# Three placements at the seam and the end of the convolution in a two-layer kernel: the second pass's w2 loads, the sums of w2, and the pace of the convolution

## The chip, the cores and the metric

The kernel runs on one core of a Trainium2 chip. The metric is the device time of one execution in microseconds (us); the profile comes from one further execution, recorded by the hardware profiler. Engines are called PE (TensorE), DVE (VectorE), ACT (ScalarE), POOL (GpSimd) and SP (SyncE, here only an issuer of DMAs). Everything is fp32.

## The reference, cut to what matters

The input x has the shape (2, 56, 56, 384): 6272 tokens of 384 channels. Two layers follow each other.

```python
# layer 0
x = x + neighborhood_attention(layer_norm(x))          # 12 heads, 7x7 windows, then a projection
y = layer_norm(x)
x = x + gelu(y @ w1 + b1) @ w2 + b2                    # 384 -> 1536 -> 384
# layer 1
h = layernorm(x)
p = h @ w_in + b_in                                    # 384 -> 768
local = depthwise_conv_3x3(p, k_conv)                  # 768 channels
mixed = 0.25 * (scan(local, rows) + scan(local, rows, reverse)
              + scan(local, columns) + scan(local, columns, reverse)) + local
mixed = layernorm(mixed)                               # over 768 channels
x = x + mixed @ w_out + b_out                          # 768 -> 384
x = x + gelu(layernorm(x) @ w1 + b1) @ w2 + b2         # own weights, 384 -> 1536 -> 384
# scan: y[i] = 0.6 * y[i-1] + 0.4 * v[i]
```

## The kernel before, in words

The tokens are 49 tiles of 128. After the attention stage, two passes go over groups of tiles. The first pass (`groups`, 13 of them, the first with one tile, the others with four) does the MLP of layer 0 and then `project_in`: it multiplies by w_in, adds the bias on ACT (L1539) and stores p, channels first, to a DRAM tensor `p_d` (L1546, on SP's queue). The second pass (`dgroups`, twelve of four tiles and one of one) does `project_out` (the product with w_out, with the layer norm of `mixed` folded in) and the MLP of layer 1. PE does all products; a hidden column is `columns` (L1205) with its copy `hidden` (L1216), a token tile is `tokens` (L1223).

The 3x3 convolution and the scans don't use PE. They run on VectorE, ScalarE and POOL's queue, beside the products of the end of the first pass and the first three groups of the second (`switch` is 3). Their work is cut into jobs. A `Band` (some lines of 128 channels) loads its part of `p_d` as `pt` (L1280, SP's queue), multiplies by the centre tap on ACT (`centre`, L1295, output `loc`), adds eight taps on VectorE (L1312), stores `loc` to `loc_d` and `mix_d` (L1320, SP's queue), scans both ways on VectorE (L1258 to L1262), scales on ACT (L1327) and accumulates into `mix_d` by an accumulating DMA on POOL's queue (L1331). A `Columns` job does the scans along the other axis: it loads `loc` (L1350), turns it on ACT (L1360), scans, turns back on ACT (L1378, output `mixed`) and accumulates. The layer norm of `mixed` needs `mix_d`, which `load_mix` loads (L1435; and the residual rows, L658).

The order is written out by hand: each engine and each DMA queue takes its instructions in the order in which the program emits them, and an instruction that waits holds all that is behind it on its engine. How the convolution is woven into the products is decided by class `Beside`: a product calls `beside.go(worth, own)` with estimated VectorE microseconds, and the class emits steps of the jobs until the debt is paid:

```python
        self.due += self.rate * worth - own
        while self.due > 0.0:
            step = self.step()
```

`beside.until(name)` emits all that is left up to a job. `rate` starts at 1.0 and is set where the last group of the first pass begins (`g == last`). The call `beside.until((1, NI - 1))` in the third group of the second pass, at its third token tile, closes the convolution.

Weights of the MLP are loaded by `weights(layer)` (L674), three DMAs of 768 KB each for w1 and for w2, on SP's queue. Layer 1's w1 goes out in the first pass, its w2 between the two passes, at the last `project_in`. ACT copies the turned and normed input of an MLP from PSUM with `channels` (L282, output `hT`); `add_row` (L1144) adds a bias row by an accumulating DMA on POOL's queue.

From the fourth group of the second pass on (`g >= switch`), the products are done as two-by-two blocks with seven products in place of eight. `hidden_by_seven` (L1657 to L1704) makes the hidden columns with sums of w1 (`more_of_w1`, L1625, on VectorE) and of the input (`sums_of_input`, L1638, `xsums`); its first three PSUM banks are opened by `open_banks` (L1237). `sums_of_hidden` (L1721 to L1723, on POOL) and four sums of w2 (`sums_of_w2`, L1715, each 128 x 1152 elements) feed `tokens_by_seven` (L1749 to L1795), the first product of which writes the bank that a tile of `project_out` has used. In these groups `project_out` takes a function `then(k)` that it calls behind each of its tiles k; its evacuation is on VectorE (L1508), its layer norm's statistics are taken on VectorE by 32x32 transposes (L1460), and the norm of the result is closed behind the last tile. `turned` (L1188) transposes the normed result on VectorE for the next group, and L1195 scales it.

Of the kernel before, what the change touches and what calls it, by code (L numbers as in the profile page):

```python
# [178 lines left out]
def block_kernel(ctx: ExitStack, tc: tile.TileContext, ins: dict, out: bass.AP):  # L179
    nc = tc.nc  # L180
# [187 lines left out]
    hT = ep.tile([P, NC, PAIR], F32, name="hT")  # L368
# [26 lines left out]
    def channels_of(n, c, bank):  # L395
        tp = bank()
        for k in range(NT):
            turn_x(n, k, c, tp)
        return lambda: take_x(n, c, tp)
# [226 lines left out]
    def project(t, bank):  # L626
        ps = bank()[:, :C]
        at = t % 7 * P
        for c in range(NC):
            nc.tensor.matmul(  # L630
                ps, lhsT=ogs[t // 7][:, c, at : at + P], rhs=wproj[:, c, :],
                start=c == 0, stop=c == NC - 1,
            )

        def add():
            if t in loaded:
                add_bias(t)
            nc.vector.tensor_tensor(xrs[t], ps, xrs[t], ALU.add)
            stores.append(("x1", x1f[t * P : (t + 1) * P, :], xrs.pop(t)))
            if t + 3 < T2 // P - 4:  # L640
                load.append(t + 3)
        return add
# [149 lines left out]
    class Dense:  # L792
# [22 lines left out]
        def step(self, j):  # L815

            due, final = self.total * (j + 1) / self.steps, j == self.steps - 1
            if self.turns and self.jobs and self.before_turns <= 1 and self.n + 3 in normal:
                self.was = True
            while True:  # L820
                ready = len(to_project) > (2 if self.n == ng - 1 else 0)
                project_next = ready and not (self.jobs and (self.was or self.n == END))
                if not project_next and not self.jobs:
                    break
                w = VAL if project_next else self.jobs[0][0]
                if self.done + 0.5 * w > due and not (final and self.jobs):
                    break
                self.done += w
                self.was = project_next
                if project_next:  # L830
                    project(to_project.pop(0), next_bank)()
                else:
                    self.jobs.pop(0)[1]()()
                    self.before_turns -= 1
            while self.turns and self.before_turns <= 0 and self.n + 3 in normal:
                channels_of(self.n + 3, self.turns.pop(0), next_bank)()
                if not final:
                    break
# [26 lines left out]
    for t in range(NS + 2):  # L865
# [17 lines left out]
        for s in fresh:  # L883
            if s % UG == 0:
                dense = Dense(s // UG)
            if s == NU - UG - 4:
# [3 lines left out]
                w1, w2, w_parts = weights(0)  # L890
# [211 lines left out]
    def passes(xs, xn, w1, w2, between=lambda ps: None):  # L1102
# [10 lines left out]
        beside = Beside()  # L1113
# [86 lines left out]
        def columns(w, m, hT, n):  # L1200

            name = "uz" if ps_m is ps_u else "mm"
            ps = ps_m.tile([P, MT], F32, name=name)
            for c in range(NC):
                nc.tensor.matmul(  # L1205
                    ps[:, : n * P], lhsT=w[:, c, m * P : (m + 1) * P], rhs=hT[:, c, : n * P],
                    start=c == 0, stop=c == NC - 1,
                )
            return ps
# [321 lines left out]
        sum_steps, seeds = [], []  # L1531
        bands = [(b, lo, hi) for b in range(B) for lo, hi in BANDS[b]]

        def project_in(g, hT, between=lambda: None, at=1):
            t0, n = groups[g]
            pt = io.tile([P, NI, MT], F32, name="mx")
            for m in range(NI):
                ps = columns(w_in, m, hT, n)
                nc.scalar.activation(  # L1539
                    pt[:, m, : n * P], ps[:, : n * P], AF.Identity, bias=col("L1_conv_b_in", m)  # L1540
                )
                beside.go(MLP)
                if m == at:
                    between()
            for b, at, here, n in images(t0, n * P):
                nc.sync.dma_start(  # L1546
                    out=p_d[b][:, :, at : at + n].rearrange("m p t -> p m t"),
                    in_=pt[:, :, here : here + n],
                )
            while bands and bands[0][0] * T1 + min(bands[0][2] + 1, H) * W <= t0 + groups[g][1] * P:  # L1550
                b, lo, hi = bands.pop(0)
                beside.jobs += [Band(b, m, lo, hi) for m in range(NI)]
                if hi == H:
                    beside.jobs += [Columns(b, m) for m in range(NI)]
# [152 lines left out]
        def sums_of_w2(w2, engine=nc.gpsimd):  # L1707

            q = NHID // 2
            b11, b12 = w2[:, :q, : C // 2], w2[:, :q, C // 2 :]  # L1710
            b21, b22 = w2[:, q:, : C // 2], w2[:, q:, C // 2 :]
            t1, t2, t3, t4 = (tp.tile([P, q, C // 2], F32, name=f"w2_t{i}") for i in range(4))
            steps = []
            for to, x, y in ((t1, b12, b11), (t2, b22, t1), (t3, b22, b12), (t4, b21, t2)):
                steps.append(lambda to=to, x=x, y=y: engine.tensor_tensor(to, x, y, ALU.subtract))  # L1715
            return (t1, t2, t3, t4), steps
# [98 lines left out]
        hT = channels(xn, groups[0][1], "L0_conv_ln2_g", "L0_conv_ln2_b")  # L1815
        add_row(x, groups[0][1], "b2_0")

        for g, (t0, n) in enumerate(groups):
# [19 lines left out]
            if g == last:  # L1838
                beside.until((0, NI - 1))
                load_row(0, "b2_1")  # L1840
                ahead = load_mix(0)
                beside.rate = 0.98
            if g < last:
                x_next, n_next = xs.pop(g + 1), groups[g + 1][1]
                norm_next = Norm(sm) if g < EARLY.stop else Ready(g + 1)
# [96 lines left out]
            if early:  # L1942
                hT = io.tile([P, NC, MT], F32, name="hT")
            elif 0 < g < last:
                hT = channels(xn_next, n_next, *ln2)
# [28 lines left out]
            if g == 0:  # L1974
                hT = channels(xn_next, n_next, *ln2)
                xsums = sums_of_input(hT)
                w2_sums, sum_steps = sums_of_w2(w2)
# [11 lines left out]
        g, x2, norm_w = waiting  # L1989
# [6 lines left out]
        hT = channels(xn, groups[g][1], *n1)  # L1996
# [5 lines left out]
        norm.shift(dgroups[0][1])  # L2002
        ahead = load_mix(1)
        w2 = w2_1
        for part in w_parts[3:]:
            part()
        project_in(g, hT, first_input)
        n2 = "L1_conv_n2_g", "L1_conv_n2_b"

        hT = channels(first["xn"], dgroups[0][1], *n2)  # L2010
        add_row(x3, dgroups[0][1], "b2_1")
        for g, (t0, n) in enumerate(dgroups[:switch]):
# [15 lines left out]
            for k in range(n):  # L2028
                if k == n - 1:
                    hT = channels(xn, dgroups[g + 1][1], *n2)  # L2030
# [20 lines left out]
        ps_y, ps_u, bank_b, banks_b = open_banks(pctx, "tail")  # L2051
        ps_m = ps_u
        xsums = sums_of_input(hT, nc.vector)
        w2_sums, sum_steps = sums_of_w2(w2)
        for step in sum_steps:
            step()
        for g, (t0, n) in enumerate(dgroups):
            if g < switch:
                continue
            if g == dlast:  # L2060
                hid = [hidden(w1, m, hT, n, "L1_conv_b1") for m in range(NHID)]
                for k in range(n):
                    ps = tokens(hid, w2, k, y_end)
                nc.vector.tensor_copy(rows[:, 1, :], x3[:, n - 1, :])
                assert n == 1 and t0 + n * P == T2
                break
            n_next = dgroups[g + 1][1]
            add_row(ahead[1], n_next, "b_out")
            s1, s2 = (tp.tile([P, NHID // 2, MT // 2], F32, name=x) for x in ("s1", "s2"))
            low, high, finish = hidden_by_seven(  # L2070
                hT, xsums, w1, w1_sums, (s1, s2), measure_by_steps(ahead, range(min(n_next, 3))),
                "L1_conv_b1",
            )
            ahead[2].close(min(n_next, 3))
            more = measure_by_steps(ahead, range(3, n_next))

            def then(k):
                if k == 0:
                    finish()
                next(more, None)  # L2080
                if k == 1 and n_next > 3:
                    ahead[2].close(n_next, first=3)

            res = x3
            x3, norm = project_out(g + 1, *ahead, then)
            if g + 2 <= dlast:
                ahead = load_mix(g + 2)
            hT = io.tile([P, NC, MT], F32, name="hT")
            for i, _ in enumerate(tokens_by_seven(low, high, s1, s2, w2, w2_sums, res, res)):
                if i == 0:  # L2090
                    norm.shift(n_next)
                    xn = normalized(norm, x3, n_next)
                if 1 <= i <= n_next:
                    turned(xn, i - 1, hT)
                if i == 5:
                    scaled(hT, n_next, *n2)
                    xsums = sums_of_input(hT) if n_next == NT else None
                    add_row(x3, n_next, "b2_1")
            nc.sync.dma_start(
                out=yout[t0 : t0 + NT * P, :].rearrange("(k p) c -> p k c", p=P), in_=res  # L2100
            )
# [8 lines left out]
    with tc.If(again > 0):  # L2110
        attention_again()
        w1, w2, w_parts = weights(0)
# [81 lines left out]
```

## Time and profile before

| | |
|---|---|
| median of three runs | 2571.08 us (2569.76 to 2578.67) |
| the profiled execution | 2575.12 us |
| its span on the core | 2573.2 us, mean granted PE clock 0.995 |
| PE busy | 2531.9 us (98%) |
| DVE busy | 1985.1 us (77%) |
| ACT busy | 1137.9 us (44%) |
| POOL busy | 585.9 us (23%) |
| waits of PE from 1600 us on | 6.2 us at 1654, 1.6 us at 1860, 3.5, 1.8 and 3.1 us between 1909 and 1930, and 1.7 us in the other three |

In the profile's lines, a name such as `L1205` is the line of the kernel before; `hT L282 <- ...` or `[6.18 <-ACT hT L282]` gives an idle time and what ended it; `SPq` is SP's DMA queue at the moment of issue; PE's granted clock is a share of full speed, and the DMA share is the mean busy share of the core's sixteen DMA engines. The first pass ends near 1660 us, the convolution near 1920 us.

### The profile page before, as it was taken

The page shows a single profiled execution, that of the slowest core. Times are in us where ns is not written, and L with a number is a line of the kernel's source. Part 1 is how long each engine was busy: PE and PEld are TensorE (multiplying, and loading weights), DVE is VectorE, ACT ScalarE, POOL GpSimd, SP SyncE. Part 2 cuts the span into 40 slices and gives each one's busy share as a digit, 9 for nine tenths or more (in the row PEclk, how much of TensorE's full clock was granted, in tenths as well). Part 3 has the DMA queues.
Part 4 walks back from the last instruction along what each step waited for, and adds up shares of the span by engine and source line. Part 5 has one row for each costly group of instructions (what it writes and reads, how often), then busy time and mean ns, then how long its engine had stood idle before and what let it go on. Part 6 is the DMA issues. An engine that isn't in the chain of part 4 may idle for free. (4 is left out here: it accounts for less than half of the span.)

```text
span 2573.2 us, 41869 instructions
## 1 busy us (share of the span) xinstructions
PE 2531.9 (98%) x16678; PEld 1734.4 (67%) x16678; DVE 1985.1 (77%) x3702; ACT 1137.9 (44%) x2058; POOL 585.9 (23%) x622
## 2 busy tenths in 40 slices
PE   9999999999999999999999999899989999999999
PEld 5666666666698887455545555455558888888888
DVE  4888978887554453899989998789887877878871
ACT  5655655654443344334455444332862233233222
POOL 0111211111442331010110002121133333333332
PEclk9999999999999999999999999999999999999999
DMA  7423454225522223467677667956890333333210
GB/s 232 152 86 99 159 174 157 86 87 195 155 65 80 68 68 95 141 175 209 178 214 281 209 186 214 250 147 168 209 238 15 74 74 74 74 74 74 47 28 21
DMA packets 155597, 342.97 MB, mean 133 GB/s; under 512 B 11158, under 2 KB 112000, under 8 KB 153088
## 3 DMA queue, kind: packets, MB, share of 16 engines
q1 hardware_dynamic: 124096, 255.65, 29.6%
q0 software_dynamic: 26352, 57.81, 13.2%
q10 hardware_dynamic: 4944, 26.74, 3.1%
q8 instruction: 133, 2.18, 0.4%
q14 instruction: 72, 0.59, 0.1%
HBM read 176.39 MB, written 134.88 MB: 121 GB/s over the span
## 5 line engine op out<-in xcount | busy, mean ns | idle before, releaser
L1312 DVE SCALAR_TENSOR_TENSOR loc<-pt,taps,loc 128x495 f32<-128x495 f32 (+13 forms) x288 | 372.9, 1295 | 35.0 <-ACT loc L1295 26.5
L1205 PE MATMUL mm<-hT,w 128*128 128x512 f32 x720 | 317.6, 596 | 6.2 <-ACT hT L282 6.2
L581 ACT ACTIVATE pts<-pts 119x448 f32<-119x448 f32 (+5 forms) x396 | 210.8, 573 | 110.6 <-DVE pts L571 100.6
L571 DVE TENSOR_TENSOR pts<-sc,bias 119x448 f32<-119x448 f32 (+5 forms) x396 | 219.0, 615 | 45.1 <-PE sc L560 44.8
L1205 PEld LDWEIGHTS mm<-hT,w 128*128 128x128 f32 x720 | 135.1, 191 | 167.7 <-issue 155.5
L1188 DVE STREAM_TRANSPOSE hT<-xn 32x96 f32<-32x96 f32 x784 | 211.2, 269 | 27.7 <-ACT xn L265 17.5
L414 PE MATMUL ps<-hT,wqkv 128*128 128x448 f32 x504 | 204.8, 550 | 2.1 <-ACT vs L459 1.5
L1460 DVE STREAM_TRANSPOSE turned<-mx 32x192 f32<-32x192 f32 x528 | 194.8, 369 | 6.9
L1223 PE MATMUL y<-w,hid 128*128 128x384 f32 x552 | 181.9, 486 | 0.0
L1223 PE MATMUL y_end<-w,hid 128*128 128x384 f32 x552 | 181.8, 486 | 0.0
L1216 ACT ACTIVATE hid<-mm,chan 128x512 f32<-128x512 f32 x120 | 82.3, 685 | 161.3 <-PE mm L1205 161.3
L1223 PEld LDWEIGHTS y_end<-w,hid 128*128 128x128 f32 x552 | 104.6, 190 | 72.1
L1223 PEld LDWEIGHTS y<-w,hid 128*128 128x128 f32 x552 | 104.3, 190 | 71.3 <-issue 0.5
L414 PEld LDWEIGHTS ps<-hT,wqkv 128*128 128x128 f32 x504 | 91.3, 189 | 84.4 <-issue 74.2
L1205 PE MATMUL mm<-hT,w_in 128*128 128x512 f32 x324 | 140.7, 593 | 0.6 <-DVE hid_u L1676 0.6
L1657 PE MATMUL ua<-hT,w 128*128 128x256 f32 x504 | 123.4, 381 | 0.0
L1331 POOL DMA_DIRECT2D mix_d<-both x36 | 32.2, 894 | 397.0 <-ACT both L1327 327.1
L560 PEld LDWEIGHTS sc<-qT,kT 32*100 32x100 f32 (+3 forms) x3168 | 87.8, 169 | 47.3 <-DVE sum L590 7.6
L600 PE MATMUL o<-pts,vt 100*32 100x112 f32 (+3 forms) x3168 | 116.3, 263 | 1.2 <-ACT pts L581 1.2
L1664 ACT ACTIVATE hid<-hid_u,chan 128x256 f32<-128x256 f32 x168 | 76.1, 500 | 88.4 <-DVE hid_u L1676 68.8
L1205 PEld LDWEIGHTS mm<-hT,w_in 128*128 128x128 f32 x324 | 61.2, 190 | 77.2 <-issue 72.9
L237 POOL TENSOR_TENSOR rs<-rs,mhalf 128x4 f32<-128x4 f32 (+4 forms) x56 | 50.2, 897 | 272.2 <-DVE rs L234 271.1
(215 smaller groups left out, 5017.1 us busy)
## 6 DMA issues: line engine op xcount, KB each, us to landing
loc<-loc_d SPq DMA_DIRECT2D x24, 784.0 KB
xa<-x_d SPq DMA_DIRECT2D x24, 768.0 KB
xa<-rows POOLq DMA_DIRECT2D x24, 768.0 KB, 11.2
bias<-in_bias_t ACTq DMA_DIRECT2D x13, 1344.0 KB
p_d<-mx SPq DMA_DIRECT2D x11, 1536.0 KB
mx<-mix_d SPq DMA_DIRECT2D x11, 1536.0 KB
v_d<-vs SPq DMA_DIRECT2D x49, 192.0 KB
xr<-in_x SPq DMA_DIRECT2D x49, 192.0 KB
```

The costliest lines, as they stand in the source:

```text
L414: nc.tensor.matmul(ps, lhsT=wqkv[:, c, m * P : (m + 1) * P], rhs=hT[:, c, half_of(n)], start=c == 0, stop=c == NC - 1,)
L560: nc.tensor.matmul(sc[i // 2][: w.keys, i % 2, q : q + TT], lhsT=kT[d, hg, w.keys_at + r * w.kc : w.keys_at + (r + w.rows) * w.kc], rhs=qT ...
L571: nc.vector.tensor_tensor(self.pts[:n, h : h + 2, lo:hi, :], sc[half][:n, :, at * TT : (at + hi - lo) * TT].rearrange("p h (c q) -> p h c ...
L581: nc.scalar.activation(t, t, AF.Exp)
L600: nc.tensor.matmul(o[i * HD : (i + 1) * HD, self.slot, :TT], lhsT=w.vt[:n, c, h * HD : (h + 1) * HD], rhs=self.pts[:n, i, c, :], start=c = ...
L1188: nc.vector.transpose(hT[j : j + HD, :, k * P + i : k * P + i + HD], xn[i : i + HD, k, :].rearrange("p (c q) -> p c q", c=NC)[:, :, j : j ...
L1205: nc.tensor.matmul(ps[:, : n * P], lhsT=w[:, c, m * P : (m + 1) * P], rhs=hT[:, c, : n * P], start=c == 0, stop=c == NC - 1,)
L1216: nc.scalar.activation(t[:, : n * P], ps[:, : n * P], AF.Gelu, bias=col(b1, m))
L1223: nc.tensor.matmul(ps, lhsT=t[:, k * P : (k + 1) * P], rhs=w[:, m, :], start=m == 0 and onto is None, stop=m == len(lhs) - 1, skip_group_c ...
L1312: nc.vector.scalar_tensor_tensor(to, pt[:, lo + dy - self.top : hi + dy - self.top, xt : xt + n], self.tap(dy, dx), to, ALU.mult, ALU.add,)
L1460: nc.vector.transpose(t[j : j + HD].rearrange("p (m c) -> p m c", m=NI)[:, :, i : i + HD], mx[i : i + HD, :, k * P + j : k * P + j + HD],)
L1657: nc.tensor.matmul(bank[:, i, :], lhsT=w[:, m * P : (m + 1) * P], rhs=x, start=start and i == 0, stop=True, skip_group_check=True,)
```

## The change

It has three parts. The rate of the convolution's weaving is 1.0 instead of 0.98 from the last group of the first pass on. The three loads of layer 1's w2 are issued behind the last `project_in` and not ahead of it: on SP's queue they now stand behind the `pt` loads and stores that this `project_in` issues and behind its store to `p_d`, and ahead of the next two `pt` loads. And the four sums of w2 are made by VectorE instead of POOL, no longer at once where the seven-product groups begin, but one behind each of the four tiles of the first such group's `project_out` (in `then(k)`, behind `finish()` at the first of them).

```diff
@@ -1839,7 +1839,7 @@
                 beside.until((0, NI - 1))
                 load_row(0, "b2_1")
                 ahead = load_mix(0)
-                beside.rate = 0.98
+                beside.rate = 1.0
@@ -2002,9 +2002,9 @@
         norm.shift(dgroups[0][1])
         ahead = load_mix(1)
         w2 = w2_1
+        project_in(g, hT, first_input)
         for part in w_parts[3:]:
             part()
-        project_in(g, hT, first_input)
@@ -2051,9 +2051,7 @@
         xsums = sums_of_input(hT, nc.vector)
-        w2_sums, sum_steps = sums_of_w2(w2)
-        for step in sum_steps:
-            step()
+        w2_sums, sum_steps = sums_of_w2(w2, nc.vector)
@@ -2077,6 +2075,8 @@
             def then(k):
                 if k == 0:
                     finish()
+                if sum_steps:
+                    sum_steps.pop(0)()
                 next(more, None)
                 if k == 1 and n_next > 3:
                     ahead[2].close(n_next, first=3)
```

## The prediction

> **What bounds the kernel now.** First the page's shares, to see which engine sets the time.
>
> ```profile
> PE 2531.9 (98%) x16678; PEld 1734.4 (67%) x16678; DVE 1985.1 (77%) x3702; ACT 1137.9 (44%) x2058; POOL 585.9 (23%) x622
> ```
>
> TensorE (PE) works 98% of the span of 2573.2 us. Its matmuls are untouched, so only its idle and slow-clock time, 41.3 us of idle in all, can change. Second, PE's waits in the second pass and the seam before it (1600 us to the end; columns: total, times, longest):
>
> ```profile
> PE mm L1205 <- ACT hT L282: 6.2, 1, 6.2
> PE yb L1237 <- ACT hT L282: 3.5, 1, 3.5
> PE uz L1657 <- DVE hid_u L1704: 3.1, 1, 3.1
> PE ub L1657 <- ACT hid_u L1696: 1.8, 1, 1.8
> PE y_end L1223 <- ACT y_end L1487: 1.6, 1, 1.6
> ```
>
> The first lies at the seam, the fifth in dgroup 2, the rest where the convolution ends. None is later than 1940. Third, windows of 5 us around the first of them (PE, PEld, DVE, ACT, POOL busy; PE's granted clock; DMA share; GB/s):
>
> ```profile
> 1655.00:1660.00 5.00, 0.00 (x0) 0.00 (x0) 2.61 (x5) 1.55 (x3) 0.00 (x0) 0.68 1.10 309
> 1660.00:1665.00 5.00, 4.60 (x9) 2.16 (x10) 2.18 (x3) 1.81 (x4) 2.23 (x2) 0.63 1.07 323
> ```
>
> PE does nothing for 5 us, and then works at a granted clock of 0.63. The same dip follows the third wait (0.67 from 1930 to 1935) and the second; the waits of 1.6 and 1.8 us show none. In the matmuls' own lengths a dip is some 3.4 us at half speed, so a stall of 3 us or more costs about 1.7 us beyond itself. Fourth, the seam in the timeline (start, length, instruction, wait), SP's queue and then ACT:
>
> ```profile
> 1645.56 0.34 SPq L1280 DMA_DIRECT2D pt<-p_d  x1
> ```
>
> ```profile
> 1658.45 0.71 ACT L1295 ACTIVATE loc<-pt,taps 128x504 f32<-128x504 f32 x1 [4.82 <-DMA pt<-p_d]
> ...
> 1659.59 2.10 ACT L282 ACTIVATE hT<-tp,chan 128x512 f32<-128x512 f32 x3
> ```
>
> w2 (three loads of 768 KB, issued from 1636.72) is ahead of a 308 KB band load pt on SP's queue, which so takes 12.9 us. ACT waits for pt, and hT's copies are queued behind it on ACT. So PE's 6.18 us are w2's.
>
> **Part 1: w2 behind the project_in.**
> Gain: pt passes ahead of w2 and lands near 1648. ACT copies hT right behind PE's transposes (1653.65 to 1655.75), and hidden column 0 ends near 1657.0 instead of 1664.68: -7.7 us, the slow clock included.
>
> What is late next: the three loads now stand on SP's queue between the p_d store and the first band load whose loc is 128x1120 (issued at 1664.03 before, used by ACT at 1674.50). That load waits for p_d to land and is then behind w2. The nearest row is in the first pass, where three w1 loads follow a p_d store:
>
> ```profile
> 1589.31 0.37 SPq L1546 DMA_DIRECT2D p_d<-mx  x1
> 1589.78 3.08 SPq L674 DMA_DIRECT2D w<-in_L_conv_w  x3
> 1594.74 0.34 SPq L1280 DMA_DIRECT2D pt<-p_d  x1
> ```
>
> That pt was in use 13.9 us after p_d's issue. Here p_d goes out at 1654.8 to 1655.3 (1653.66 before; it is now behind stores that wait for VectorE's taps, done at 1654.2): pt at 1668 to 1670 by this row. But POOL's queue carries an accumulation of a band and two of rows (768 KB each) in the same time, and two queues share packet by packet. The queue lines of 1921 to 1926 show it:
>
> ```profile
> q0 software_dynamic: 377, 0.58, 65.5%
> q1 hardware_dynamic: 377, 0.77, 46.0%
> ```
>
> 1.8 MB at 0.58 MB in 5 us (0.116 MB/us) is 15 us of sharing, in which SP's queue gets 0.77/5 x 15 = 2.3 MB of its 4.8 MB (stores 0.25, p_d 1.57, w2 2.36, pt 0.6); the other 2.5 MB at about 0.39 MB/us (first-pass loads) take 6.4 us: 1655 + 15 + 6.4 = 1676. Another way: the DMA share is over 1 here, so the same bytes end later by the time in which the queue now lacks work, about 1649 to 1654: the load, landed at 1671.3 before, comes near 1676.5. I take 1677, with 1668 and 1680 as ends.
>
> ACT wants it after the third hidden column's copy, near 1663.5; PE has three banks and goes on to column 5, which ends at 1671.9. Then loc (1.22) and hid (0.69) run from 1677.0 to 1678.9, and column 6 starts at 1679.1, with 1.7 us of slow clock to follow: 1680.8 against 1679.5 before. So a 7 us stall replaces the 6 us stall. **Seam: +1.5 us** (from -7.7, if it lands by 1670, to +4).
>
> **Part 2: pace.** Rate 1.0 for 0.98 counts from 1541, where the second pass's work begins: 2% of 364 us is 7.3 us more convolution in the order by 1905. VectorE has room (41 busy of 50 us at 1850 to 1900). Two effects. In dgroup 2, seven ACT blocks of 3.1 us instead of six stand before the seeds of L1487, so y_end's wait of 1.57 becomes about 3.4: **+1.8** (0 to +4.5 with a slow clock). And at the end of the convolution fewer scans remain behind the last token tiles:
>
> ```profile
> 1907.62 3.12 ACT L1378 ACTIVATE mixed<-line 128x392 f32<-128x392 f32 x4 [3.54 <-DVE line L1262]
> ...
> 1910.54 2.07 ACT L282 ACTIVATE hT<-tp,chan 128x512 f32<-128x512 f32 x3
> ...
> 1912.43 3.81 DVE L1638 TENSOR_TENSOR xsums<-xsums,hT 128x256 f32<-128x256 f32 x1
> ...
> 1912.65 3.30 POOL L1715 TENSOR_TENSOR w_t<-w 128x1152 f32<-128x1152 f32 x1
> ```
>
> hT waited on ACT for a mixed block, that for a scan. With the last block ahead of hT, the 3.46 us go. The 1.82 us (ACT L1696 held for an accumulation of mix_d, 4.32) go because that leaves some 7 us earlier.
>
> **Part 3: sums of w2.** The four POOL subtractions go from there. VectorE's four xsums then take 4 x 0.43 = 1.7 us instead of 9.9 (1911.97 to 1921.86), L1704 comes early, and its 3.15 us go. With both slow stretches (1912.8 to 1916.2, 1929.9 to 1933.3; 1.65 each): 3.46 + 1.82 + 3.15 + 3.3 = **-11.7** (-7 to -12).
>
> Their new place is not free. A VectorE sum of 768 columns took 0.96 us (L1625), so 1152 columns take 1.43, four 5.7 us. VectorE last waits for PE at 1954.65 (L1676, 1.96); from there to the norm's close at 1967.80 it idles 0.7 us only. So the close comes 5.0 us later. L1508 of tile 2, done at 1965.04, is passed by two sums and ends near 1967.7, while PE wanted its bank at 1966.06: +1.7. Then xn, 64 transposes and L1195 run dense, and the first xsums (done 1993.11 on POOL, read by PE at 1994.23) comes at 1997.8, where PE after its first wait would read it at 1995.9: +1.9. **+4.2** with some 0.3 us of latency in each (+2 to +7).
>
> One rule speaks against this placing. The rows above: xsums went from 0.43 us (the first, at 1911.97) to 3.81 beside POOL's sum, and POOL's 2.8 us are what 1.27 us for 512 columns (L1721) scale to, so VectorE alone paid. The Trainium skill ("SBUF — State Buffer", section "SBUF: two separate sides") says that the shared port pair is locked for a whole instruction, and whichever starts second is blocked. By the page POOL's L1722 and L1723 (1955.19 to 1957.68) would also wait behind the first moved sum, 1.43 us each at most; by the row only VectorE waits, up to 1.2 us. Sum 4.2 without a meeting, 5.4 with one. I keep 4.2, as one of four sums meets them, and 7 as upper end.
>
> **Sum.** +1.5 +1.8 -11.7 +4.2 = -4.2 us on the profiled 2575.12 us (0.16%), whose span is 2573.2 with 1.9 around it. It lies between the runs' 2571.08 median and their highest, 2578.67, so I put the difference on the median: 2567.
>
> **Rivals.**
> (a) *No new stall at the band load.* POOL's rows finish early enough and pt lands by 1670. For: 13.9 us in the first pass. Against: the shared queues and a DMA share over 1. Seam -7.7: sum -13.4, 2557.7 (-10 to -19).
> (b) *Slower: w2 holds the band load.* Each us of landing after 1677 costs PE one. From 1681.2 on the change loses, from 1694 by over 12.9 us, the 0.5% that a measurement of this kernel can tell from no change. For: p_d goes out late and everything is behind it in one queue. Against: the bytes end near 1676 by two counts. At 1688: +7, 2578.
> (c) *The end doesn't move.* Extra pace turns into waits on ACT (L1360 and L1378 were already what scans waited for), so hT stays late; only the POOL sums' 3.15 + 1.65 go. +1.5 +1.8 -4.8 +4.2 = +2.7, 2574.
>
> **How the numbers follow.** Forecast 0.50 (2561 to 2574), (a) 0.20, (b) 0.18, (c) 0.12. The range 2553 to 2583 takes in (a) but its far end, and (b) up to a landing of 1693. Faster by over 0.5%: 0.6 of (a) and a little of the forecast, 0.16. Slower by over 0.5%: 0.4 of (b), some of (c) with the slow clock in dgroup 2 and the upper end in the tail, and costs of parts that I see no row for, 0.18. Within: 0.66.
>
> **What would show it.** Right: no 6.2 us wait on hT; ACT L1295 128x1120 waiting 12 to 14 us for pt<-p_d, and PE idle 7 us before column 6, near 1672; no waits of yb, ub, uz at the end of the convolution, xsums at 0.43, clock 1.0 there; PE short waits of 1 to 3 us at L1749's first product and at the next group's first xsums. Wrong: the band load landing by 1670, hT still behind a mixed block near 1910, or no PE wait behind the moved sums.

## The result, and the profile after

The changed kernel takes 2573.99 us (median of 12 runs, 2571.48 to 2578.93) against 2574.8 us before (12 runs on the same chip): ratio 1.0001, interval 0.999 to 1.0011. No difference. Its profiled span is 2573.4 us against 2573.2. The zero is a sum, as the trace shows: the end of the convolution is 9.9 us shorter, three other stretches are together 10.1 us longer, and the seam, where one stall took the place of another, is about as long as it was.

TensorE's share first, then all waits of PE from 1600 us on in the changed kernel (total, times, longest):

```profile
PE 2535.8 (99%) x16678; PEld 1736.1 (67%) x16678; DVE 1982.8 (77%) x3706; ACT 1137.3 (44%) x2058; POOL 575.4 (22%) x618
```

```profile
PE mm L1205 <- ACT hid L1216: 4.2, 1, 4.2
PE y_end L1223 <- ACT y_end L1487: 4.0, 1, 4.0
PE xi L1448 <- DVE st L221: 2.7, 1, 2.7
PE y L1749 <- DVE xc L1508: 2.3, 1, 2.3
PE ub L1657 <- issue: 2.2, 1, 2.2
```

The 6.2 us on hT are gone, and 4.2 us on hid stand in their place; y_end's 1.6 us became 4.0; xi is new in this size; hT's 3.5 and uz's 3.1 us at the end of the convolution are gone; and a wait of L1749 appears where there was none. ub's stayed (1.8 before, 2.2 now).

PE's instructions stand in nearly the same order in both kernels, so the time between two of its marks can be compared. "Turning" is PE's transposing of a group's normed input (L279). The start is the turning behind the last project_in (1652.75 us before, 1653.08 after), and there are five stretches: the seam (from the start to the first tile of dgroup 0's project_out), dgroup 1 (from the turning of its input to the second tile of its project_out), dgroup 2 (from the turning of its input to the fourth tile of its project_out), the end of the convolution (from the turning of dgroup 3's input to the second tile of its project_out), and the tail (from there to the second product of tokens_by_seven). The stretches between them took the same time in both (38.7, 34.8 and 27.1 us). This table, in us, holds all kernels that were run:

| kernel | seam | dgroup 1 | dgroup 2 | end | tail | sum against before |
|---|---|---|---|---|---|---|
| before | 42.9 | 47.7 | 56.0 | 54.5 | 15.5 | |
| changed | 42.5 | 49.4 | 60.2 | 44.6 | 19.7 | -0.2 |
| w2 moved alone | 40.2 | 47.7 | 56.0 | 54.4 | 15.5 | -2.7 |
| pace alone | 36.6 | 49.4 | 60.0 | 52.5 | 15.5 | -2.6 |
| sums alone | 43.0 | 47.7 | 56.0 | 49.7 | 19.7 | -0.5 |
| changed, w2 behind the band loads | 35.2 | 50.8 | 60.1 | 44.6 | 19.7 | -6.1 |
| changed, sums in gaps | 40.5 | 51.1 | 60.8 | 44.6 | 15.5 | -4.1 |
| pace and sums, w2 as before | 36.6 | 49.4 | 59.5 | 44.7 | 19.7 | -6.6 |
| three mends | 35.2 | 51.0 | 54.2 | 47.1 | 15.5 | -13.5 |
| three mends, three rates | 35.3 | 47.3 | 54.2 | 49.9 | 15.5 | -14.5 |

Each row is one profiled execution. How far such rows scatter can be seen where two kernels have the same code: "changed" and "sums in gaps" differ only behind dgroup 2, and yet by 2.0 us in the seam and 1.7 us in dgroup 1. The sums also leave out what lies ahead of the start, so they differ from the differences of the medians by up to 3.7 us.

Now the lines. The seam in the changed kernel, SP's queue and then ACT, VectorE and PE in the timeline (start, length, instruction, wait):

```profile
1654.00 0.37 SPq L1546 DMA_DIRECT2D p_d<-mx  x1
1654.47 5.77 SPq L674 DMA_DIRECT2D w<-in_L_conv_w  x3
1663.86 2.19 SPq L1280 DMA_DIRECT2D pt<-p_d  x2
```

```profile
1674.78 1.23 ACT L1295 ACTIVATE loc<-pt,taps 128x1120 f32<-128x1120 f32 x1 [10.71 <-DMA pt<-p_d]
1675.91 0.67 ACT L1216 ACTIVATE hid<-mm,chan 128x512 f32<-128x512 f32 x1
1676.04 4.19 DVE L1312 SCALAR_TENSOR_TENSOR loc<-pt,taps,loc 128x1100 f32<-128x1100 f32 x3 [9.82 <-ACT loc L1295]
...
1676.63 5.49 PE L1205 MATMUL mm<-hT,w 128*128 128x512 f32 x6 [4.25 <-ACT hid L1216]
```

p_d's landing releases the band load at 1663.86; it is then behind w2 and is used 10.9 us later. ACT holds 10.71 us for it, hid is behind it on ACT, and PE, out of banks, stands 4.25 us and runs its next column at the slow clock (six matmuls in 5.49 us; column 0 took 2.84). VectorE holds too: its taps had been waiting 9.82 us when they started at 1676.04.

Dgroup 1: first a window of 20 us in the kernel before (PE, PEld, DVE, ACT, POOL busy; PE's granted clock; DMA share; GB/s), then VectorE in the kernel before, then VectorE and PE in the changed kernel:

```profile
1740.00:1760.00 20.00, 19.24 (x61) 9.75 (x61) 19.61 (x19) 6.17 (x8) 2.27 (x2) 1.00 0.86 228
```

```profile
1752.15 1.02 DVE L221 BATCH_NORM_STATS2 st<-xi 128x6 f32<-128x384 f32 x2
...
1753.34 2.44 DVE L1258 TENSOR_TENSOR_SCAN both<-decay,loc 128x1120 f32<-128x1120 f32 x1
```

```profile
1749.19 2.49 DVE L1258 TENSOR_TENSOR_SCAN both<-decay,loc 128x1120 f32<-128x1120 f32 x1
...
1754.36 1.00 DVE L221 BATCH_NORM_STATS2 st<-xi 128x6 f32<-128x384 f32 x2
...
1754.95 0.55 PE L1448 MATMUL xi<-ident,mx 128*128 128x128 f32 x3 [2.72 <-DVE st L221]
```

VectorE was full here already (19.61 of 20 us). The scans of a band stood behind the statistics of xi and now stand ahead of them, and the second half of xi on PE waits for the statistics of the first.

The end of the convolution, in the timeline of all engines:

```profile
1907.41 3.14 ACT L1378 ACTIVATE mixed<-line 128x392 f32<-128x392 f32 x4 [0.95 <-DVE line L1262]
...
1910.77 2.10 ACT L282 ACTIVATE hT<-tp,chan 128x512 f32<-128x512 f32 x3
...
1912.24 0.42 DVE L1638 TENSOR_TENSOR xsums<-hT 128x256 f32<-128x256 f32 x1 [3.00 <-ACT hT L282]
1912.70 0.43 DVE L1638 TENSOR_TENSOR xsums<-xsums,hT 128x256 f32<-128x256 f32 x1
...
1914.86 0.33 PE L1237 MATMUL yb<-zeros 128*128 128x384 bf16 x1
```

hT is copied at the same time as before (1910.77 against 1910.54). It is PE that comes 5.8 us later (it turns dgroup 3's input at 1905.81 against 1899.99), so in this kernel the wait is gone because the time was lost ahead of it, not because hT came sooner. The second sum of xsums takes 0.43 us, not 3.81: that gain is real.

The tail, PE in the kernel before and then all engines in the changed kernel:

```profile
1966.06 4.06 PE L1749 MATMUL y<-w,hid 128*128 128x192 f32 x24
```

```profile
1951.12 1.27 POOL L1722 TENSOR_TENSOR s<-s,hid 128x512 f32<-128x512 f32 x1
1951.19 2.41 DVE L1715 TENSOR_TENSOR w_t<-w 128x1152 f32<-128x1152 f32 x1
...
1952.35 2.38 POOL L1723 TENSOR_TENSOR hid<-hid 128x512 f32<-128x512 f32 x1
...
1957.94 1.33 DVE L1715 TENSOR_TENSOR w_t<-w,w_t 128x1152 f32<-128x1152 f32 x1
...
1963.75 0.61 DVE L1508 SCALAR_TENSOR_TENSOR xc<-y,rs,xa 128x384 f32<-128x384 f32 x1
...
1964.41 5.85 PE L1749 MATMUL y<-w,hid 128*128 128x192 f32 x24 [2.25 <-DVE xc L1508]
```

Two sums stand ahead of tile 2's evacuation (L1508) on VectorE, PE wants that bank 2.25 us before it is free, and then runs 24 matmuls in 5.85 us instead of 4.06. The first sum met POOL's and both paid: VectorE took 2.41 us, where the other three sums took 1.32 to 1.33, and POOL's L1723 2.38, where it took 1.26 before.

### The profile page after: what moved, and what is told of

Its sections match the earlier page's. It is cut to its first block, busy times and chain, and to the rows that moved or that the text cites. A ratio compares the mean times of both kernels' runs of the same rounds, so it can differ in the third digit from the quotient of the medians.

```text
span 2573.4 us, 41871 instructions
## 1 busy us (share of the span) xinstructions
PE 2535.8 (99%) x16678; PEld 1736.1 (67%) x16678; DVE 1982.8 (77%) x3706; ACT 1137.3 (44%) x2058; POOL 575.4 (22%) x618
## 6 DMA issues: line engine op xcount, KB each, us to landing
xa<-rows POOLq DMA_DIRECT2D x24, 768.0 KB, 11.9
```

## The experiments

The kernel before was run again beside these: a median of 2574.4 us (37 runs) for the four kernels up to "w2 behind the two band loads", of 2575.42 us (17 runs) for the other four. The diffs are cut, `...` marking what is left out.

**One part at a time.** Three kernels make one part of the change each, to see which part owns which stretch of the table. A rival was that the later waits (xi, y_end) are the seam's debt: VectorE, held for the band load, never catches up.

w2 alone:

```diff
         w2 = w2_1
+        project_in(g, hT, first_input)
         for part in w_parts[3:]:
             part()
-        project_in(g, hT, first_input)
```

> Only the w2 loads are moved; pace 0.98, sums of w2 on POOL as before. Theory A (each part has its own places, as in the ledger of lags: seam -0.4, dgroups 1 and 2 +5.8, end of the convolution -9.9, tail +4.2): the seam changes as in the changed kernel (no 6.2 us wait on hT, a 3 to 5 us wait behind the 128x1120 band load), within -3 to +2 us; y_end's wait stays about 1.6, no 2.7 us wait of xi at 1752, the three waits at the end of the convolution stay (3.5, 1.8, 3.1). Total -3 to +2 us. Theory B (the later waits are the seam's: VectorE, held 9.8 us for the band load, stays behind its order): xi's 2.7 us and a y_end wait near 4 us appear here too, total +4 to +8 us.

Measured: ratio 0.9989 (0.998 to 0.9999), 2573.05 us. PE's waits from 1600 us on, the first five:

```profile
PE yb L1237 <- ACT hT L282: 3.5, 1, 3.5
PE xi L1448 <- DVE st L221: 2.7, 3, 1.9
PE ub L1657 <- ACT hid_u L1696: 2.6, 1, 2.6
PE uz L1657 <- DVE hid_u L1704: 2.4, 1, 2.4
PE y_end L1223 <- ACT y_end L1487: 1.6, 1, 1.6
```

y_end's 1.6 us is as before, and xi's 2.7 us are three waits of which the one in dgroup 1 is 0.52, as before (0.51). The longest, 1.89 us, is the seam's: the band load held ACT for 6.72 us and VectorE for 7.8, and PE stood behind that, with some 1.7 us of slow clock to follow. The wait on hT in the seam fell from 6.2 to 1.3 us. So the move alone gains 2.7 us in the seam. Although VectorE was held, xi and y_end in dgroups 1 and 2 are as before: the later waits are not the seam's debt. VectorE was held 2 us less than in the changed kernel; the next run, where it is held 4.0 us only and the waits are there, settles it.

Pace alone:

```diff
-                beside.rate = 0.98
+                beside.rate = 1.0
```

> Only the rate 1.0; w2 ahead of the band load and the sums of w2 on POOL as before. Theory A: xi's wait near 1752 (2 to 3 us) and y_end's near 1861 (4 us and its slow clock) are here: +5.8 us; at the end of the convolution the 3.5 us wait on hT and its slow clock go (-5), the waits of ub (1.8) and uz (3.1 with slow clock) stay because the sums are still beside VectorE's xsums; the tail is unchanged. The extra order also puts the band's centre tap ahead of the last project_in's last copy, so p_d's store can be held behind the band load: seam 0 to +5. Total +1 to +6 us. Theory B: dgroups 1 and 2 as before, total -5 to 0.

Measured: 0.9993 (0.9982 to 1.0005), 2573.44 us. PE's waits, the first three:

```profile
PE uz L1657 <- DVE hid_u L1704: 4.9, 1, 4.9
PE y_end L1223 <- ACT y_end L1487: 3.8, 1, 3.8
PE xi L1448 <- DVE st L221: 2.7, 1, 2.7
```

xi and y_end are the pace's, as theory A said (dgroups 1 and 2 together +5.6 us against before), and the rival fell. At the end of the convolution -5 was expected and -2.0 came: hT's wait is gone, but with POOL's sums still beside xsums uz's wait grew from 3.1 to 4.9 us and PE waited 1.7 us for xsums. What was not expected is the seam (0 to +5): 36.6 us, 6.3 shorter than before and shorter than with the move, with w2 still ahead. ACT in the timeline of this run:

```profile
1656.09 0.72 ACT L1295 ACTIVATE loc<-pt,taps 128x504 f32<-128x504 f32 x1 [2.10 <-DMA pt<-p_d]
...
1657.79 2.11 ACT L282 ACTIVATE hT<-tp,chan 128x512 f32<-128x512 f32 x3
...
1671.65 1.23 ACT L1295 ACTIVATE loc<-pt,taps 128x1120 f32<-128x1120 f32 x1 [3.66 <-DMA pt<-p_d]
```

In this run the turning on PE starts at 1655.68. The small band load was issued 10.4 us ahead of that (7.2 before) and in use 0.4 us behind it (5.7 before). The higher rate has brought the steps at the seam forward by about one: on SP's queue a band's two loc stores now go out ahead of p_d (1655.25 and 1657.92), where before they followed it (1654.25 and 1653.66). PE waited 1.46 us for hT and not at all for the second load: w2 had been issued 26 us ahead of it, and it was in use 7.4 us after its issue.

Sums alone:

```diff
-        w2_sums, sum_steps = sums_of_w2(w2)
-        for step in sum_steps:
-            step()
+        w2_sums, sum_steps = sums_of_w2(w2, nc.vector)
...
             def then(k):
                 if k == 0:
                     finish()
+                if sum_steps:
+                    sum_steps.pop(0)()
```

> Only the sums of w2 on VectorE behind the tiles of project_out; w2's loads and the pace as before. Theory A: seam, dgroups 1 and 2 as before; the 3.5 us wait on hT stays, uz's 3.1 us and its slow clock go (-4.8), in the tail a wait of about 2.3 us on L1508 with a slow stretch (+4.2): total -2 to +1 us. Rival (the tail's wait comes from the shifted timing after the faster end, not from the sums): no wait at L1749's first product, total -5.

Measured: 1.0001 (0.9993 to 1.0009), 2575.38 us. One of PE's waits:

```profile
PE y L1749 <- DVE xc L1508: 2.3, 1, 2.3
```

The end is 4.8 us shorter and the tail 4.2 us longer: the tail's cost comes without the other two parts. As the end is shorter here too, this run can't tell the sums from the earlier arrival; the run with the sums in VectorE's gaps can, as its end is as short as the changed kernel's and its tail is not longer.

**w2 behind the two band loads.** If the queue is the cause of the new stall, w2 need only go one place further back.

```diff
         project_in(g, hT, first_input)
-        for part in w_parts[3:]:
-            part()
+        w_parts = w_parts[3:]
...
                 hid.append(hidden(w1, m, hT, n, "L1_conv_b1"))
                 beside.go(MLP, measure_beside(m, g + 1, ahead))
+                if m >= 4 and w_parts:
+                    w_parts.pop(0)()
```

> The changed kernel with the three w2 loads issued behind the next two band loads and one pair of loc stores instead of ahead of them (one each behind hidden columns 4, 5 and 6 of the first group of the second pass). If w2 in the queue is what holds the 128x1120 band load: it lands near 1668 instead of 1674.8, PE's 4.25 us wait and its slow clock go, -5 to -6 us against the changed kernel. Theory B: xi's 2.7 us go with them, and y_end's wait falls to about 2: -9 to -12. Theory A: xi's and y_end's waits stay. If it is POOL's rows and the late p_d that hold it: landing at 1673 or later, no gain.

Measured: 0.9964 (0.9951 to 0.9978), 2564.63 us. SP's queue and ACT in its timeline:

```profile
1665.56 0.99 SPq L1280 DMA_DIRECT2D pt<-p_d  x2
...
1668.02 3.16 SPq L674 DMA_DIRECT2D w<-in_L_conv_w  x3
```

```profile
1670.63 1.23 ACT L1295 ACTIVATE loc<-pt,taps 128x1120 f32<-128x1120 f32 x1 [4.20 <-DMA pt<-p_d]
```

The load is in use 5.1 us after its issue instead of 10.9, PE doesn't wait, and the seam is 35.2 us: 7.3 less than in the changed kernel, where 5 to 6 had been expected. xi and y_end stay: again they are the pace's. So w2 in the queue is what held the band load; the rows of POOL's queue, which go out 0.5 us ahead of p_d in both kernels, don't do it without w2.

**The sums in VectorE's gaps.** The same four sums on the same engine, elsewhere in its order.

```diff
         w2_sums, sum_steps = sums_of_w2(w2, nc.vector)
+        for _ in range(2):
+            sum_steps.pop(0)()
...
             ahead[2].close(min(n_next, 3))
+            if sum_steps:
+                sum_steps.pop(0)()
...
             def then(k):
+                if sum_steps:
+                    sum_steps.pop(0)()
                 if k == 0:
                     finish()
-                if sum_steps:
-                    sum_steps.pop(0)()
```

> The changed kernel with the four sums of w2 still on VectorE but moved to gaps of its trace: two right behind xsums (VectorE then waits 3.35 us for an accumulation), one behind the close of the first three tiles (2.55 us idle there), one ahead of finish() (1.96 us idle). If the tail's 2.25 us wait and slow clock come from the sums between the norm's statistics: the wait of L1749 goes, tail as before, -4.2 us against the changed kernel. Rival (VectorE is simply full in this group): 2 us or more of waits stay.

Measured: 0.9977 (0.9965 to 0.9989), 2569.35 us. All of PE's waits from 1600 us on:

```profile
PE y_end L1223 <- ACT y_end L1487: 3.8, 1, 3.8
PE mm L1205 <- ACT hid L1216: 3.5, 1, 3.5
PE xi L1448 <- DVE st L221: 2.7, 1, 2.7
PE ub L1657 <- issue: 2.2, 1, 2.2
```

L1749's wait is gone and the tail is 15.5 us, with the end at 44.6 as in the changed kernel. The four sums took 1.33 to 1.36 us each. VectorE was not full: what cost time was the place of the sums, between the norm's statistics.

**Pace and sums, w2 as before.** The changed kernel with the move of w2 undone: its loads are ahead of project_in again.

```diff
+        for part in w_parts[3:]:
+            part()
         project_in(g, hT, first_input)
-        for part in w_parts[3:]:
-            part()
```

> The changed kernel with w2's loads put back ahead of the last project_in: pace 1.0 and sums on VectorE alone. The run with the pace alone had a seam 6.3 us shorter than before with w2 still ahead, so if the seam's stall was already removed by the pace and w2's move then only brings in the new one: seam 36.6 us from the turning of the last input to the first w_out tile (42.5 in the changed kernel), xi 2.7, y_end 4, end and tail as in the changed kernel: -5.9 us against the changed kernel, about -6 against before. Rival (the seam's length in that run was an accident of the first pass's timing): seam 41 to 43, no gain.

Measured: 0.9967 (0.9954 to 0.9979), 2566.43 us. The seam is 36.6 us against 42.5 in the changed kernel: with the pace at 1.0, moving w2 behind the project_in costs 5.9 us. The seam is as long as in the run of the pace alone, so that was no accident of timing. Two of the change's three parts, without the third, are 0.3% faster than the kernel before.

**A version that beats both.** Three mends: w2 behind the band loads, the sums in the gaps (both as above), and the two seeds of L1487 ahead of two of ACT's blocks:

```diff
-                if m == NHID - 1:
+                if m == NHID - 3:
                     seeds = [seed_out(*ahead[1:], k) for k in range(2)]
```

> Three mends together: w2's loads behind the two band loads (-7.2 in the seam against the changed kernel), sums in VectorE's gaps (-4.2), and the two seeds of L1487 put out behind hidden column 8 instead of 10, ahead of two of ACT's blocks (y_end's 4.0 and its slow clock go, -5.8). xi's 2.7 us stay. Sum -17 against the changed kernel if they add; if the time saved at y_end comes back as a wait on hT at the end of the convolution (VectorE's scans then being late by as much): -11 to -13.

Measured: 0.9942 (0.9928 to 0.9956), 2561.56 us. Two waits of PE are left:

```profile
PE xi L1448 <- DVE st L221: 2.7, 1, 2.7
PE ub L1657 <- issue: 2.6, 1, 2.6
```

This is 0.6% below the kernel before. Against the changed kernel the table has -13.3 us where -17 was expected if the mends add up. No wait on hT came back. Dgroup 2 is 6.0 us shorter than in the changed kernel; 2.5 us of that are given back at the end, in a slow stretch of the clock behind ub's wait, and 1.6 us in dgroup 1, where xi's wait is the same but the clock fell behind it.

Then the rate by group:

```diff
         for g, (t0, n) in enumerate(dgroups[:switch]):
+            beside.rate = 1.03 if g == switch - 1 else 0.98
```

> As the kernel with the three mends, but the rate is 1.0 only at the seam, 0.98 in the first two groups of the second pass and 1.03 in the third. If xi's wait is VectorE's order running ahead of what it can do in those groups: xi's wait falls from 2.7 to below 1 us, -2 against the kernel with the three mends. Against it: less is done by the end, so a wait on hT near 1910 comes back, up to +5.

Measured: 0.9941 (0.9928 to 0.9953), 2560.46 us, no measurable gain over the three mends alone. xi's wait falls to 0.6 us and dgroup 1 is 3.7 us shorter, as expected of an order that asks less; at the end 2.8 us come back (a 1.3 us wait on a seed, 0.5 on hT, ub's at 3.6).

## Why the prediction was right or wrong

The forecast was no measurable difference as the likeliest outcome, with a stall that moves and a new cost in the tail, and that is what came. The time alone says little: the range of 30 us held the middle of each of the three rivals as well. The median was forecast 7 us too low. 3.7 us of this are the base, as 2571.08 was the median of three runs and twelve runs before gave 2574.8. The rest lies in the four terms, one of which was right and three were off:

- *Seam, +1.5: measured -0.4.* The first half came as worked out: hidden column 0 ends 4.3 us behind the turning instead of 11.9, so -7.6 against -7.7. The new stall is there as drawn, with w2 between p_d and the band load, and was put too high: ACT waited 10.71 us where 12 to 14 were forecast, the load was in use at 1674.8 where 1677 was taken, and PE stood 4.25 us instead of 7, with 2.7 us of slow clock instead of 1.7. What it had wrong is what the first half belongs to. "PE's 6.18 us are w2's" holds in the trace of before, and w2's move alone brings the end of column 0 to 5.4 us. But the pace alone brings it to 5.6. With the pace in place (the run with pace and sums), w2's move gains 1.4 us ahead of column 0's end and loses 7.2 behind it. The pace was costed at the end and in dgroup 2 only; what it does at the seam was left out. The row from the first pass was also misread: the load issued at 1594.74 is first used at 1605.01, 15.7 us after p_d's issue and not 13.9. Only the low end of the landing (1668 to 1670) rests on this row, and not the 1677 that was taken.
- *Dgroups 1 and 2, +1.8: measured +5.8.* y_end's wait went to 4.0 and not 3.4, and with the slow clock behind it dgroup 2 cost 4.2, near the upper end that was given. xi's 2.72 us in dgroup 1 (+1.7) were missed: at the higher rate a band's scans stand ahead of xi's statistics on VectorE, and xi's second half waits. "VectorE has room" was read from another stage: at 1850 to 1900 it was busy 41 of 50 us, but from 1740 to 1760 it was busy 19.6 of 20 us before the change already.
- *End, -11.7: measured -9.9.* uz's wait went as worked out, with xsums at 0.43 us. ub's 1.82 us did not go (2.19): the accumulation that ACT waits for leaves at 1910.90 against 1911.11, not 7 us earlier. And hT did not come sooner. Against the turning of the last input, the first xsums starts at 259.2 us in both kernels. In the run with the pace alone it starts at 253.1, and with w2 behind the band loads at 253.2. So the pace does bring hT some 6 us forward, as forecast; the changed kernel lost this lead at the seam, where VectorE was held 9.8 us for the band load against 4.0 and 3.3 in those runs. (With the sums in the gaps it was held 9.1 us, and xsums starts at 259.5.) Rival (c) had hT late too, but for another reason (waits on ACT), and it had the wait stay; here PE's own delay covered it.
- *Tail, +4.2: measured +4.2.* L1508 of tile 2 came 2.25 us late and not 1.7 (2.0 with latency); the 2.2 us expected on xsums did not come, and 1.8 us of slow clock came instead. The sum is right, its second half by luck.

On the lock of the shared port, the rule and the row that were weighed: the first moved sum met POOL's L1722 and L1723, and VectorE and POOL each paid about 1.1 us. "VectorE alone paid" did not carry over; the rule of the Trainium skill ("SBUF — State Buffer", section "SBUF: two separate sides") that the second to start is blocked fits both lengths (2.41 and 2.38 us): VectorE's sum started 0.07 us behind L1722, and L1723 then started while that sum was still running.

## What to carry to other kernels

When several edits aim at the same stall, price each with the others in place: here the pace had already removed most of what moving w2 was to remove, and the move then cost 5.9 us. A load that is taken out of one consumer's way stands in another's; put it behind the next loads that someone waits for, not just behind the one that hurt. Work moved to an engine with idle time must go into its gaps, ahead of a wait that it has anyway; four sums of 1.33 us cost 4.2 us among the statistics of a norm and nothing in gaps of the same group.

## What was not expected of the hardware

The clock falls after shorter waits than had been read from the trace of before, where 3.15 us was the shortest, and not after all of them. These are all waits of PE of 1.2 us and more between 1640 and 2010 us, in the ten profiles:

| wait of PE | how many | with a slow clock behind it |
|---|---|---|
| 1.25 to 1.82 us | 9 | 0 |
| 1.89 to 2.73 us | 19 | 10 |
| 3.15 to 6.18 us | 15 | 15 |

The slow clock cost 1.7 us in most cases, and up to 2.9 behind the longer waits. In the middle row, length does not decide: in the tail, 2.25 us slowed the clock in all four kernels that had that wait, ub's 2.12 to 2.57 us in none of six (2.64 us in a seventh did), and the same wait of xi, 2.71 to 2.73 us, in three kernels and not in three others. Windows of 5 us around it in the changed kernel, and then around it with the sums in the gaps (PE, PEld, DVE, ACT, POOL busy; PE's granted clock; DMA share; GB/s):

```profile
1750.00:1755.00 5.00, 2.28 (x9) 1.01 (x7) 4.93 (x5) 1.86 (x3) 0.00 (x0) 1.00 1.07 264
1755.00:1760.00 5.00, 5.00 (x14) 2.43 (x15) 4.90 (x8) 0.69 (x1) 0.00 (x0) 1.00 0.88 244
```

```profile
1745.00:1750.00 5.00, 2.28 (x10) 1.04 (x9) 4.93 (x5) 1.71 (x2) 0.00 (x0) 1.00 1.08 277
1750.00:1755.00 5.00, 5.00 (x11) 2.22 (x10) 4.90 (x8) 0.34 (x1) 0.00 (x0) 0.66 0.80 223
```

Dgroup 1 is 49.4 us in the one and 51.1 in the other for this alone (the clock was 1.00 there and 0.66 here). The Trainium skill ("TensorE: Matmul & The Clock Gate", section "What's actually happening") has the activity window free-running, which would make it a matter of where the wait falls in the window; the runs here show both outcomes but not the window, so what decides stays open. In this kernel a wait of 2 to 3 us is thus to be priced with and without some 1.7 us of slow clock.
